# Cross-attention and a dequantised feed-forward on one core: the first block's steps in a new order, and three of down's integer steps in earlier rounds

## The chip, the core and the metric

The kernel runs on one core of a Trainium2 chip. The metric is the device time of one execution in microseconds; it is given as the median of several runs. The engines are PE (matrix products, with PEld for its weight loads), DVE (vector work), ACT (activation functions, scaled copies), POOL (general elementwise work, and one queue of transfers) and SP (a second queue of transfers).

## What is computed

`x` has 32 batches of 64 rows and 512 columns, and so has the context. First comes cross-attention. Its "channels" are the 64 rows of a batch; the 512 columns are cut into 8 heads of 64. Then comes a gated feed-forward over the 512 columns, whose three weights are stored as integers 0 to 15 with a zero point and a scale for each group of 128 input rows. Both parts add to `x`.

```python
h = layernorm(x)                                   # over 512 columns
q, k, v = Wq@h + bq, Wk@ctx + bk, Wv@ctx + bv      # 64x64 weights, per batch
p = softmax(q_head @ k_head.T / 8)                 # 64x64 per batch and head
x = x + Wo @ concat(p @ v_head) + bo
W = (integers - zeros) * scales                    # gate, up: 512x1792; down: 1792x512
h = layernorm(x)
x = x + (silu(h @ W_gate) * (h @ W_up)) @ W_down
```

## The kernel before

**Tiling.** Two batches make a pair: 128 partitions of 512 columns. Two pairs make a set, four pairs a block, and there are four blocks. The feed-forward of a block works on 512 columns (its 4 x 128 rows, transposed). The normalised input is held transposed in a high half `hTh` and a low half `hTl`, and each product is taken with both halves. The 1792 inner columns are 14 chunks of 128. Gate and up of a chunk take four groups `g` of 128 input rows. Between the groups ACT multiplies the running sum in PSUM by a quotient of two scales (`s_q`, line 670), so the weights stay integers less their zero points. Down adds each chunk's product to `y` on DVE, times a scale (line 718); it has four column tiles `l` per chunk, and only two PSUM banks (`ps_d`) for these products.

**Getting the weights.** Integers come by POOL's queue (`load_wide`, line 271, `load_down`, line 275), in four column ranges `wide`: 0 to 256, then three of 512. Zero points come as broadcasts by SP's queue (`load_zeros`, `load_down_zeros`). POOL subtracts zeros from gate and up (`weight_steps`, line 309), DVE from down (`down_steps`, line 322).

**The first block.** Its attention and second normalisation run pair by pair before any feed-forward product, in the order of the string `START` (line 796): each word is a step of a pair ("2.scores") or a shared step. `tc.manual_schedule()` keeps each engine's instructions in that order. The steps of a pair are: `stats`, `scale`, `apply` (mean and variance on DVE, inverse root on POOL, normalise on DVE at line 112); `q`, `k`, `v` products and `q_out`, `k_out` (add the bias from PSUM on DVE, line 450), `v_out` (ACT); `scores`, `highest`, `less`, `exp`, `sums`, `divide` (the softmax: PE, DVE, DVE, ACT, DVE, POOL); `turn`, `turn_out`, `weigh` (products with Wo and v); `residual` (line 568: two DVE operations of 128x256, product + bias + x, then a store to `x1_dram`); `stats2`, `scale2`, `apply2`, `flip` (transpose), `high` (ACT), `low` (DVE). `warm` is a pair of products with no use but to keep PE running. Shared steps: `gate`, `up`, `more_gate`, `more_up` issue weight loads, `integers` does one subtraction of 256 columns on POOL, `zeros`, `broadcast`, `more` bring the zero points, `scales` and `quotients` build `s_q`. "behind products" ties a transfer to the last product traced before it.

**The rounds.** After that come 28 rounds per block (line 938 on). A round advances two chains of gate and up, one step of the next block's attention (`ROUND_STEPS`; for the next two blocks' sets the names end in `_4to`, `_6to`, and so on), and down, which lags by 6 rounds and does two of its four column tiles twice per round. `LOADS_AT` names the rounds that load weights, `WEIGHTS_AT` those in which POOL subtracts, `DOWN_AT` those in which DVE subtracts the zeros of one more chunk of down. A planner then sets each engine's order from its own estimates; `tc.issue_after` holds some instructions behind the newest one traced on their engine.

Of the kernel before, what the change touches and what calls it, by code (L numbers as in the profile page):

```python
# [9 lines left out]
F32 = mybir.dt.float32  # L10
# [16 lines left out]
def kernel(  # L27
# [88 lines left out]
    with ExitStack() as fast:  # L116
# [118 lines left out]
            yield  # L235
            nc.scalar.copy(s_all, pS)

        def quotients():

            s_inv = early.tile([P, 2, NS - FC], F32, tag="s_inv", name="s_inv")  # L240
            later = s_all[:, 0:2, FC:]
            nc.vector.scalar_tensor_tensor(s_inv, later, 0.0, later, ALU.is_equal, ALU.add)
            nc.vector.reciprocal(s_inv, s_inv)
            nc.vector.tensor_tensor(s_q, s_all[:, 0:2, : NS - FC], s_inv, ALU.mult)

        def last_quotients():

# [102 lines left out]
        class Attention:  # L350
# [61 lines left out]

            stats2, scale2 = stats, scale

            def apply2(self):

                if not PB <= self.p < 2 * PB:
                    return self.apply()
                less = small.tile([P, self.n], F32, tag="less", name=f"less_{self.name}")
                nc.vector.scalar_tensor_tensor(  # L420
                    less, self.mv[:, :, 0], -1.0, self.rs, ALU.mult, ALU.mult
                )
                for i in range(self.n):
                    nc.scalar.activation(
                        self.at["xn"][:, i, :],
                        self.x[:, i, :],
                        AF.Identity,
                        bias=less[:, i : i + 1],
                        scale=self.rs[:, i : i + 1],
                    )  # L430

# [22 lines left out]

            def k_out(self):
                self.with_bias("k_eT", self.pk, 1)

            def q(self):
                self.pq = self.heads("xn", WQ, "pq")
# [103 lines left out]

            def residual(self):
                x_heads = self.by_head(self.x)
                for h in range(2):
                    x_h = x_heads[:, :, h, :]
                    nc.vector.scalar_tensor_tensor(
                        x_h, self.po[:, h, :, :], bvo[:, 1:2], x_h, ALU.add, ALU.add
                    )  # L570
                nc.sync.dma_start(x1_dram[:, self.p : self.p + self.n, :], self.x)


            def flip(self):
                two = self.tile("ph")[:, : self.n, :]
                self.ph = two.rearrange("p i (c d) -> p c i d", d=P)
                for i in range(self.n):
                    for c in range(KT):
                        nc.tensor.transpose(
                            self.ph[:, c, i, :], self.at["xn"][:, i, ts(c, P)], ident  # L580
                        )

# [206 lines left out]
        def chain(*gens):  # L789
# [4 lines left out]


        START = """
            0.stats 0.scale 0.apply 1.stats projections 1.scale biases
            projections_out 1.apply 2.stats 0.k biases_out 2.scale 3.stats 0.q 1.q
            0.k_out 3.scale 0.q_out 1.k zeros 1.q_out 0.scores 1.k_out 2.k 3.apply
            1.scores broadcast 0.highest 2.apply 2.k_out 0.less 0.v 1.highest 0.exp  # L800
            2.q 1.less 0.v_out 3.q 0.sums 1.exp 2.v 2.q_out 0.divide 3.k gate
            2.v_out 1.sums 2.scores 3.q_out 1.divide 3.k_out 1.v 2.highest 3.scores
            1.v_out 2.less 1.turn 3.highest 2.exp 0.turn up rows 3.less 1.turn_out
            2.sums 3.exp 1.weigh 0.turn_out 3.sums 2.divide 3.v 1.residual 1.stats2
            3.divide integers integers integers integers 0.weigh 3.v_out 2.turn
            0.residual 0.stats2 1.scale2 more_gate integers 3.turn more 2.turn_out
            2.weigh 3.turn_out 1.apply2 0.scale2 integers integers scales 2.residual
            2.stats2 3.weigh scales_out 1.flip 2.warm 3.residual 3.stats2 3.warm
            3.warm 2.scale2 integers 1.high 0.apply2 3.scale2 more_up 2.apply2
            0.flip 1.low 2.flip 3.apply2 0.high quotients 3.flip 3.warm 2.high 0.low  # L810
            3.high 2.low 3.low
        """
        place = places(att)
        with (
# [44 lines left out]
            for step in START.split():  # L859
                if step[0].isdigit():  # L860
                    getattr(pairs[int(step[0])], step[2:])()
                elif step == "zeros":
                    zeros_to_dram()
                elif step == "broadcast":
                    with behind_products():
                        early_zeros.append(load_zeros(*wide[0], early))
                elif step == "gate":
                    with behind_products():
                        load_wide(ng, gate_rows, *wide[0])
                elif step == "up":  # L870
                    with behind_products():
                        load_wide(nu, up_rows, *wide[0])
                elif step == "rows":
                    with behind_products():
                        load_rows(PB // SET)
                elif step == "more":
                    with behind_products():
                        early_zeros.append(load_zeros(*wide[1]))
                elif step == "more_gate":
                    load_wide(ng, gate_rows, *wide[1])  # L880
                elif step == "more_up":
                    load_wide(nu, up_rows, *wide[1])
                    load_down(0, wide[1][0] + wide[1][1])
                elif step == "integers":
                    next(weights)
                elif step == "quotients":
                    quotients()
# [47 lines left out]
        with ExitStack():  # L935
            for r in range(NBLK * ROUNDS + LAG):
# [163 lines left out]
```

## Time and profile before

| what | value |
|---|---|
| three runs | 437.92 us median (437.63 to 438.35) |
| the profiled execution | 437.77 us, its span 436.0 us |
| PE busy in the span | 406.6 us (93%) |
| DVE, ACT, POOL busy | 327.9, 307.7, 281.1 us |
| first product of the feed-forward | starts at 39.54 us |
| mean granted PE clock | 0.992 |

All times of the profile count from the start of the span; about 1.8 us of the execution lie outside it. In a table by stage the columns are: the stage, its length, each engine's busy time with its number of instructions, the granted PE clock as a share of full speed, the share of time that the transfer engines were busy, and GB/s. A line of a timeline is: start, duration, engine, source line, operation, output and inputs with their shapes, the count, and in brackets the idle time before it and what ended that. Consecutive instructions of an engine overlap, so the next one starts some 0.1 us before the last one's end.

### The profile page before, as it was taken

To read this page: it belongs to the slowest core of one execution; us is meant where nothing else is said; L and a number is where in the kernel's file an instruction comes from. 1 tells how busy PE (TensorE), PEld (TensorE's weight loads), DVE (VectorE), ACT (ScalarE), POOL (GpSimd) and SP (SyncE) were. 2 spreads that over 40 slices of the span, in tenths; PEclk is the share of its full clock that TensorE was granted. 3 is DMA by queue.
4 is the path that set the end of the run, shared out by engine and by line. 5 is a ranking of instruction groups with operands and counts; after the bars stand their busy time and mean duration, and the time that the engine had idled before them with its cause. 6 is when DMAs were issued, how large, how long until landed. Compare 5 with 4: busy or idle time off the path is not lost. (4 is left out here: it accounts for less than half of the span.)

```text
span 436.0 us, 10361 instructions
## 1 busy us (share of the span) xinstructions
PE 406.6 (93%) x4191; PEld 312.6 (72%) x4191; DVE 327.9 (75%) x513; ACT 307.7 (71%) x472; POOL 281.1 (64%) x291
## 2 busy tenths in 40 slices
PE   4767989899999999999999999989999999999993
PEld 3555657567777776877778787767778888887772
DVE  4988766997788874895779785896869656768675
ACT  2243888476978589766988579666788778777771
POOL 4384948867645446675778668775787887774330
PEclk9999989999999999999999999999999999999998
DMA  7299648951021200411010102300000013110002
GB/s 214 63 301 370 209 126 284 322 187 50 2 74 50 98 2 0 146 51 51 0 50 1 51 2 98 112 34 2 2 37 15 1 49 98 59 39 0 2 4 100
DMA packets 20911, 36.54 MB, mean 84 GB/s; under 512 B 1832, under 2 KB 7416, under 8 KB 20856
## 3 DMA queue, kind: packets, MB, share of 16 engines
q1 hardware_dynamic: 14056, 24.20, 16.6%
q0 software_dynamic: 6192, 11.01, 8.4%
q8 instruction: 35, 0.57, 0.5%
q10 hardware_dynamic: 608, 0.59, 0.4%
q14 instruction: 20, 0.16, 0.1%
HBM read 27.37 MB, written 8.42 MB: 82 GB/s over the span
## 5 line engine op out<-in xcount | busy, mean ns | idle before, releaser
L718 DVE SCALAR_TENSOR_TENSOR y<-pd,s_all,y 128x512 f32<-128x512 f32 x204 | 150.0, 743 | 43.2 <-PE pd L708 39.8
L670 ACT ACTIVATE pg<-pg,s_q 128x512 f32<-128x512 f32 x168 | 111.7, 666 | 67.0 <-PE pg L660 65.9
L670 ACT ACTIVATE pu<-pu,s_q 128x512 f32<-128x512 f32 x168 | 111.2, 663 | 8.0 <-PE pu L660 6.9
L686 POOL CAST hh<-h 128x512 fp32r<-128x512 f32 x55 | 37.0, 673 | 100.4 <-DVE h L676 89.1
L705 PE MATMUL pd<-hh,nd 128*128 128x512 f32 x224 | 93.2, 416 | 2.3 <-DVE y L718 1.6
L660 PE MATMUL pg<-hTh,ng 128*128 128x512 f32 x224 | 90.3, 403 | 3.2 <-DVE hTl L602 1.6
L660 PE MATMUL pu<-hTh,nu 128*128 128x512 f32 x224 | 90.7, 405 | 1.4 <-POOL nu L309 1.1
L660 PE MATMUL pg<-hTl,ng 128*128 128x512 f32 x224 | 89.3, 399 | 0.0
L660 PE MATMUL pu<-hTl,nu 128*128 128x512 f32 x224 | 89.1, 398 | 0.0
L708 PE MATMUL pd<-hl,nd 128*128 128x512 f32 x224 | 88.8, 396 | 0.0
L687 POOL TENSOR_TENSOR hl<-h,hh 128x512 fp32r<-128x512 f32 x55 | 72.7, 1321 | 4.2
L676 DVE SCALAR_TENSOR_TENSOR h<-pu,s_all,g 128x512 f32<-128x512 f32 x56 | 41.8, 747 | 29.7 <-ACT g L673 19.6
L339 POOL TENSOR_TENSOR squares<-squares 128x512 f32<-128x512 f32 (+1 forms) x46 | 55.1, 1198 | 1.7
L705 PEld LDWEIGHTS pd<-hh,nd 128*128 128x128 f32 x224 | 42.0, 188 | 18.0 <-DVE y L718 5.2
L660 PEld LDWEIGHTS pg<-hTh,ng 128*128 128x128 f32 x224 | 42.3, 189 | 16.9 <-ACT pg L670 2.6
L660 PEld LDWEIGHTS pu<-hTh,nu 128*128 128x128 f32 x224 | 42.3, 189 | 16.6 <-ACT pu L670 2.0
L660 PEld LDWEIGHTS pg<-hTl,ng 128*128 128x128 f32 x224 | 42.4, 189 | 9.5
L660 PEld LDWEIGHTS pu<-hTl,nu 128*128 128x128 f32 x224 | 42.4, 189 | 9.4
L673 ACT ACTIVATE g<-pg,s_all 128x512 f32<-128x512 f32 x56 | 39.0, 697 | 13.6 <-PE pg L660 12.1
L708 PEld LDWEIGHTS pd<-hl,nd 128*128 128x128 f32 x224 | 42.1, 188 | 8.3 <-issue 0.4
L309 POOL TENSOR_TENSOR nu<-nu,z 128x512 fp32r<-128x512 f32 (+1 forms) x16 | 17.5, 1095 | 3.0 <-DMA nu<-in_L_ffn_up_w_dram 2.9
L309 POOL TENSOR_TENSOR ng<-ng,z 128x512 fp32r<-128x512 f32 (+1 forms) x16 | 16.7, 1050 | 2.4 <-DMA ng<-in_L_ffn_gate_w_dram 2.4
(295 smaller groups left out, 464.9 us busy)
## 6 DMA issues: line engine op xcount, KB each, us to landing
c_set<-in_ctx_dram SPq DMA_DIRECT2D x6, 512.0 KB
x<-in_x_dram SPq DMA_DIRECT2D x6, 512.0 KB
z<-z_dram SPq DMA_DIRECT2D x6, 512.0 KB
ng<-in_L_ffn_gate_w_dram POOLq DMA_DIRECT2D x3, 1024.0 KB, 7.1
nu<-in_L_ffn_up_w_dram POOLq DMA_DIRECT2D x3, 1024.0 KB, 8.0
x_dram<-x SPq DMA_DIRECT2D x6, 512.0 KB
r<-x_dram SPq DMA_DIRECT2D x6, 512.0 KB
out_dram<-r SPq DMA_DIRECT2D x6, 512.0 KB
```

Source lines behind the costliest of these rows:

```text
L309: nc.gpsimd.tensor_tensor(piece, piece.bitcast(F32), z16[:, m, g, :], ALU.subtract)
L339: nc.gpsimd.tensor_tensor(total[:, :n], total[:, :n], square[:, :n], ALU.add)
L660: nc.tensor.matmul(acc, w[:, g, ts(f, P)], half[:, g, :], start=(g == 0 and half is hi), stop=(g == KT - 1 and half is lo), skip_group_che ...
L670: nc.scalar.activation(acc, acc, AF.Copy, scale=by)
L673: nc.scalar.activation(g_sb, acc, AF.Silu, scale=by)
L676: ins = nc.vector.scalar_tensor_tensor(h_sb, acc, by, g_sb, ALU.mult, ALU.mult)
L686: nc.gpsimd.tensor_copy(hh, h_sb)
L687: ins = nc.gpsimd.tensor_tensor(hl, h_sb, hh.bitcast(F32), ALU.subtract)
L705: nc.tensor.matmul(pd, w, h_hi[t, f], start=(t, f) != LAST, stop=False, skip_group_check=True)
L708: nc.tensor.matmul(pd, w, h_lo[t, f], start=False, stop=True, skip_group_check=True)
L718: ins = nc.vector.scalar_tensor_tensor(y, pd, by, y, ALU.mult, ALU.add)
```

## The change

Two changes are made at once.

*The first block.* `START` is a new order: pairs go 0, 2, 1, 3 for much of it, and the queries are computed before the keys for pair 0. The work of some steps goes to other engines. Pairs 2 and 3 are normalised by POOL (`apply_pool`). Their keys are copied from PSUM by ACT (`k_copy`), and POOL adds the bias (`k_bias`). The output bias is added to `x` early, by ACT (`shift`), so that the residual is one DVE operation of 128x512. The second normalisation is done by ACT in the first block too (`apply2`, line 424 before), after a small DVE operation (`less2`). The quotients' guards against zero are two POOL operations, and the quotients of the first two chunks are made in the first block, those of the other twelve after round 1. The transposes of `flip` are kept together. The eight `integers` are spread differently, and all four subtractions of up's first columns stand directly before `more_up`.

*Down's integers.* The steps of chunks 3, 4 and 5 are taken in rounds 8, 8 and 9; before they were in rounds 9, 11 and 13. The order listing of the two programs shows on DVE: chunks 3 and 4 now stand before the second y of chunk 1, chunk 5 behind h of chunk 3. On SP the zero broadcast for chunks 6 to 9 now stands before a store of `x`. On PE the order of the rounds is the same up to the fourth down product of chunk 3, which now comes earlier; a few products behind it change places.

```diff
-        def quotients():
-            s_inv = early.tile([P, 2, NS - FC], F32, tag="s_inv", name="s_inv")
+        s_inv = const.tile([P, 2, NS - FC], F32, tag="s_inv", name="s_inv")
+        def guards():
             later = s_all[:, 0:2, FC:]
-            nc.vector.scalar_tensor_tensor(s_inv, later, 0.0, later, ALU.is_equal, ALU.add)
-            nc.vector.reciprocal(s_inv, s_inv)
-            nc.vector.tensor_tensor(s_q, s_all[:, 0:2, : NS - FC], s_inv, ALU.mult)
+            nc.gpsimd.tensor_scalar(s_inv, later, 0.0, None, ALU.is_equal)
+            nc.gpsimd.tensor_tensor(s_inv, s_inv, later, ALU.add)
+        def quotients(fs: slice):
+            for m in range(2):
...
+                nc.vector.reciprocal(inv, inv)
+                newest["DVE"] = nc.vector.tensor_tensor(quot, num, inv, ALU.mult).ins
...
+            def apply_pool(self):
+                nc.gpsimd.tensor_scalar(
+                    self.at["xn"][:, 0, :], self.x[:, 0, :], self.mv[:, 0, 0:1], self.rs,
+                    ALU.subtract, ALU.mult)
+            def less2(self):
+                self.less = small.tile([P, self.n], F32, tag="less", name=f"less_{self.name}")
+                nc.vector.scalar_tensor_tensor(
+                    self.less, self.mv[:, :, 0], -1.0, self.rs, ALU.mult, ALU.mult)
             def apply2(self):
-                if not PB <= self.p < 2 * PB:
+                if self.p >= 2 * PB:
                     return self.apply()
...
+            def k_copy(self):
+                nc.scalar.copy(self.by_bank("k_eT"), self.pk)
+            def k_bias(self):
+                k = self.by_bank("k_eT")
+                b = bqk[:, 1, :].unsqueeze(1).unsqueeze(1).to_broadcast([P, 2, self.n * KT, D])
+                nc.gpsimd.tensor_tensor(k, k, b, ALU.add)
...
             def residual(self):
                 x_heads = self.by_head(self.x)
+                if self.n == 1:
+                    x_h = x_heads.rearrange("p n h d -> p h n d")
+                    nc.vector.tensor_tensor(x_h, self.po, x_h, ALU.add)
+                    return self.keep_rows()
...
+            def shift(self):
+                nc.scalar.activation(self.x, self.x, AF.Identity, bias=bvo[:, 1:2])
...
         START = """
...
+            0.stats 0.scale 0.apply projections 1.stats biases projections_out
+            1.scale 2.stats 0.q biases_out 0.shift 3.stats 2.scale 0.k 2.apply_pool
+            0.q_out 2.k 0.k_out 3.scale 2.shift 2.q 1.apply 3.apply_pool 2.k_copy
+            0.scores 2.q_out 1.shift 1.k 0.highest zeros 3.shift 0.less 1.q 2.k_bias
+            broadcast 1.k_out 0.exp 3.k 1.q_out 2.scores 3.k_copy 0.sums 1.v 3.k_bias
+            2.highest 3.q 1.v_out 1.scores 2.less 0.divide gate 3.q_out 2.exp 0.v
+            1.highest 0.turn 0.v_out 3.scores 0.turn_out 1.less 2.sums 1.exp 2.v 3.v
+            2.v_out 3.highest 2.divide up rows 0.weigh 3.v_out 3.less 1.sums 3.exp
+            2.turn 2.turn_out 3.sums 1.divide 2.weigh 0.residual 3.divide 1.turn
+            2.residual scales 1.turn_out 2.stats2 integers 3.turn more scales_out
+            integers 1.weigh 3.turn_out 0.stats2 2.scale2 3.weigh 0.warm integers
+            2.less2 3.residual 2.apply2 0.scale2 3.stats2 2.flip integers 2.high
+            more_gate 0.less2 1.residual 0.apply2 guards 1.stats2 0.flip 1.warm
+            3.scale2 0.high 2.low 1.scale2 3.less2 integers 1.less2 3.apply2 0.low
+            integers 1.apply2 quotients 3.flip integers 3.high 1.flip integers 3.low
+            1.high more_up 1.low 1.warm
...
-        DOWN_AT = [4, 5, 6, 14, 22] + [2 * f + 3 for f in range(2, FC)]
+        DOWN_AT = {4: 1, 5: 1, 6: 1, 7: 1, 8: 2, 9: 1, 14: 1, 22: 1}
+        DOWN_AT |= {2 * f + 3: 1 for f in range(6, FC)}
...
-                    if r in DOWN_AT:
-                        advance(down_weights)
+                    advance(down_weights, DOWN_AT.get(r, 0))
...
+                if r == 1:
+                    with tc.issue_after(newest["DVE"]):
+                        quotients(slice(FIRST // P, FC))
```

More of the change, by code (lines that the diff above doesn't have):

```diff
@@ L236, in scales @@
             nc.scalar.copy(s_all, pS)
-        def quotients():
-            s_inv = early.tile([P, 2, NS - FC], F32, tag="s_inv", name="s_inv")
+        s_inv = const.tile([P, 2, NS - FC], F32, tag="s_inv", name="s_inv")
+        def guards():
             later = s_all[:, 0:2, FC:]
-            nc.vector.scalar_tensor_tensor(s_inv, later, 0.0, later, ALU.is_equal, ALU.add)
-            nc.vector.reciprocal(s_inv, s_inv)
-            nc.vector.tensor_tensor(s_q, s_all[:, 0:2, : NS - FC], s_inv, ALU.mult)
+            nc.gpsimd.tensor_scalar(s_inv, later, 0.0, None, ALU.is_equal)
+            nc.gpsimd.tensor_tensor(s_inv, s_inv, later, ALU.add)
+        def quotients(fs: slice):
+            for m in range(2):
+                inv, num, quot = (
+                    a.rearrange("p (g f) -> p g f", f=FC)[:, :, fs]
+                    for a in (s_inv[:, m, :], s_all[:, m, : NS - FC], s_q[:, m, :])
+                )
+                nc.vector.reciprocal(inv, inv)
+                newest["DVE"] = nc.vector.tensor_tensor(quot, num, inv, ALU.mult).ins
         def last_quotients():
@@ L413 @@
             stats2, scale2 = stats, scale
+            def apply_pool(self):
+                nc.gpsimd.tensor_scalar(
+                    self.at["xn"][:, 0, :],
+                    self.x[:, 0, :],
+                    self.mv[:, 0, 0:1],
+                    self.rs,
+                    ALU.subtract,
+                    ALU.mult,
+                )
+            def less2(self):
+                self.less = small.tile([P, self.n], F32, tag="less", name=f"less_{self.name}")
+                nc.vector.scalar_tensor_tensor(
+                    self.less, self.mv[:, :, 0], -1.0, self.rs, ALU.mult, ALU.mult
+                )
             def apply2(self):
-                if not PB <= self.p < 2 * PB:
+                if self.p >= 2 * PB:
                     return self.apply()
[L419 to L422, printed above, removed]
+                if self.n > 1:
+                    self.less2()
                 for i in range(self.n):
@@ L427, in apply2 @@
                         AF.Identity,
-                        bias=less[:, i : i + 1],
+                        bias=self.less[:, i : i + 1],
                         scale=self.rs[:, i : i + 1],
@@ L570, in residual, with keep_rows @@
                     )
+                self.keep_rows()
+            def keep_rows(self):
                 nc.sync.dma_start(x1_dram[:, self.p : self.p + self.n, :], self.x)
+            def shift(self):
+                nc.scalar.activation(self.x, self.x, AF.Identity, bias=bvo[:, 1:2])
             def flip(self):
@@ L576, in flip @@
                 self.ph = two.rearrange("p i (c d) -> p c i d", d=P)
[L577 to L581, printed above, removed]
+                with self.in_order() as first_taken:
+                    for i in range(self.n):
+                        for c in range(KT):
+                            nc.tensor.transpose(
+                                self.ph[:, c, i, :], self.at["xn"][:, i, ts(c, P)], ident
+                            )
+                            first_taken()
             def warm(self):
@@ L796 @@
         START = """
[L797 to L808, printed above, removed]
@@ L809 @@
-            3.warm 2.scale2 integers 1.high 0.apply2 3.scale2 more_up 2.apply2
-            0.flip 1.low 2.flip 3.apply2 0.high quotients 3.flip 3.warm 2.high 0.low
-            3.high 2.low 3.low
+            0.stats 0.scale 0.apply projections 1.stats biases projections_out
+            1.scale 2.stats 0.q biases_out 0.shift 3.stats 2.scale 0.k 2.apply_pool
+            0.q_out 2.k 0.k_out 3.scale 2.shift 2.q 1.apply 3.apply_pool 2.k_copy
+            0.scores 2.q_out 1.shift 1.k 0.highest zeros 3.shift 0.less 1.q 2.k_bias
@@ L886 @@
                 elif step == "quotients":
-                    quotients()
+                    quotients(slice(0, FIRST // P))
+                elif step == "guards":
+                    guards()
                 elif step.endswith("_out"):
```

## The prediction

> **What bounds the kernel now.** I read the page's slices first, then busy time by stage, then the timelines of PE, VectorE (DVE) and GpSimd (POOL) from 0 to 112 us. The chain of work that ended last says nothing here: it holds only the last 0.4%.
>
> ```profile
> core 0: us, PE busy (x) PEld busy (x) DVE busy (x) ACT busy (x) POOL busy (x), PEclk, DMA share, GB/s
> 0.00:39.50 39.50, 24.84 (x717) 19.75 (x717) 32.21 (x72) 12.10 (x22) 22.03 (x41) 1.00 0.71 219
> 39.50:110.00 70.50, 66.08 (x754) 47.01 (x755) 53.17 (x75) 50.28 (x75) 51.27 (x49) 0.98 0.65 206
> 110.00:400.00 290.00, 286.70 (x2592) 223.55 (x2591) 218.74 (x334) 226.22 (x345) 200.19 (x196) 1.00 0.13 42
> ...
> 60.00:63.40 3.40, 3.40 (x9) 2.49 (x9) 2.76 (x6) 2.20 (x5) 2.12 (x2) 0.51 0.18 44
> ```
>
> From 110 us on PE is 99% busy, so a shift of PE's position at 110 us moves the end by as much. Up to 39.5 us DVE is the full engine (32.2 us, with 1.9 us of gaps from 8.5 us on) and ACT the empty one (12.1). Between them lie about 4.4 us of PE gaps, and one stretch at half clock (last row).
>
> ```profile
> 39.54 0.47 PE L660 MATMUL pg<-hTh,ng 128*128 128x512 f32 x1 [1.56 <-DVE hTl L602]
> ...
> 47.14 1.48 PE L438 MATMUL pq_4to<-w_T,xn_set 64*64 64x64 f32 x64
> ...
> 69.51 0.50 PE L705 MATMUL pd<-hh,nd 128*128 128x512 f32 x1
> ...
> 83.41 0.50 PE L705 MATMUL pd<-hh,nd 128*128 128x512 f32 x1 [1.28 <-DVE y L718]
> ...
> 89.36 0.49 PE L660 MATMUL pu<-hTh,nu 128*128 128x512 f32 x1 [0.84 <-POOL nu L309]
> ```
> ```profile
> 37.41 1.88 DVE L602 TENSOR_TENSOR hTl<-ph,hTh 128x512 fp32r<-128x512 f32 x3
> ...
> 45.19 2.68 DVE L112 TENSOR_SCALAR xn_set<-x,mv_4to,rs_4to 128x512 f32<-128x512 f32 x2 [2.09 <-POOL rs_4to L402]
> ...
> 66.46 1.85 DVE L322 TENSOR_TENSOR nd<-nd,z 128x512 fp32r<-128x512 f32 x1
> 68.23 0.57 DVE L398 TENSOR_SCALAR rs_6to<-mv_6to 128x2 f32<-128x2 f32 x1
> 68.72 1.40 DVE L718 SCALAR_TENSOR_TENSOR y<-pd,s_all,y 128x512 f32<-128x512 f32 x2
> ```
> ```profile
> 35.19 0.81 POOL L273 DMA_DIRECT2D nu<-in_L_ffn_up_w_dram  x1
> ...
> 43.31 1.17 POOL L309 TENSOR_TENSOR nu<-nu,z 128x512 fp32r<-128x512 f32 x1 [2.94 <-DMA nu<-in_L_ffn_up_w_dram]
> 44.43 0.72 POOL L402 TENSOR_TENSOR rs_4to<-rs_4to,nhalf 128x2 f32<-128x2 f32 x1
> ...
> 65.83 1.93 POOL L529 TENSOR_TENSOR q_e_set<-q_e_set,sm_4to 128x1024 f32<-128x1024 f32 x1
> ```
>
> What to see: the first gate product (39.54) follows DVE's last low half (37.41 + 1.88 = 39.29) by 0.25. The second set's queries (47.14) hang on a DMA: nu's second columns land at 43.3, POOL subtracts, POOL takes the root (44.43), DVE normalises (45.19), and PE, free at 47.05, starts at 47.14. So this chain is already just in time. And the fourth down product of chunk 1 (69.51) starts as DVE's y (68.72 + 0.74 = 69.46) ends: also just in time.
>
> **The first block, step by step.** Durations are start to start in a full queue. DVE gives up: two normalisations (pairs 2, 3; 0.46 each, 0.9), two key biases (0.60 each, 1.2), four second normalisations (0.46 each, 1.8), half of each residual (0.82 for two 128x256 becomes one 128x512 from PSUM like L450's 0.60: 0.9), and 0.65 of the quotients (1.15 becomes four tiny operations, 0.5). It gains four "less" of 128x1; the near row is L420 (128x2): 0.15 alone, 0.40 beside POOL; I take 0.25, 1.0 in all. Net 4.5 us off DVE.
>
> The work goes to ACT and POOL. ACT: four bias shifts (near row: exp 128x512, 0.63), two key copies (0.57), four normalisations (L424: 0.82), 7 us into an engine 27 us idle. POOL: two normalisations, two key biases (near row L529: 1.05 each) and two guard operations of 84 columns (0.3 each from L309's 0.66 for 256 columns), 4.8 us into an engine 17 us idle. Bounds for the unshown POOL normalisation: 0.61 (cast row) to 2.0. A rule speaks against this move: the Trainium skill's "GPSIMD Engine Reference", section 4, wants elementwise work on VectorE, because GpSimd takes about twice as long for two inputs. The rows agree on the price (1.05 against 0.60). By the rule alone the two biases and two normalisations would cost 2 us more than they save; by the rows of the queues they replace time of the full engine by time of one that waits 6.2 us before its first division (18.40). With 2.0 us each the walk below ends 0.6 later, no more.
>
> I then walk the new order forward, each engine in its own order, each step at the latest of its inputs and its engine. The same walk over the old order gives 39.13 for the last low half (trace 39.29), so I add 0.16. New stations: first scores at 12.3 as before; last softmax sums at 23.7 (before 25.1); residuals of pairs 0 and 2 at 24.9; pair 3's at 28.1, pair 1's at 30.3; pair 1's statistics at 31.4 (+1.10), root 32.05 (+0.56), less 32.9, ACT's two normalisations 33.4 and 34.1 (0.82, 0.72 apart), transpose 34.75, high half 35.4, low half 36.1. Plus 0.16 and 0.25: first gate product at 36.5, **3.0 us earlier** (2.2 if every less waits 0.65 for POOL, 3.8 if none waits). 1.5 of the 4.5 stay as new DVE waits: the end is now a chain through ACT. The transfers that these steps issue move with them: first gate columns 19.4 to 17.8, first up columns 23.3 to 21.8, ng's second columns 29.5 to 28.6, all on POOL's queue behind products that end earlier; the stores of the residuals on SP's. The remaining quotients (0.9 in round 1) lie in DVE's idle 2.09 before 45.19.
>
> **Does the start survive the second set?** With 3.0 off, PE wants the queries at 44.1. The chain from nu's landing to PE was 47.14 - 43.31 = 3.8, so nu must land by 40.3. Its issue hardly moves (35.19 to 34.6: four subtractions at 0.64 now stand right before it). What changes is the traffic before it. In the old trace the zero broadcast (1 MB, issued at 28.15) ran until 34 at 0.2 MB/us, POOL's queue moved nothing from 29 to 33, ng landed at 39.1, nu took 4.1 more. In the new order the broadcast stands behind pair 3's turn (25.7 instead of 27.2) and earlier stores: issued at 25.8, done near 32; ng then needs 1 MB at 0.4 MB/us plus 0.5 MB of stores and rows: near 36; nu (and half of a row load) 1.3 to 1.5 MB more: 39.5 to 41. I take 40.3: the 3.0 just survives. Bounds: 39.5 (no wait) to 43.3 (all is given back).
>
> **Down's integers.** Chunks 3 to 5 leave rounds 9, 11, 13 for 8, 8, 9. In DVE's order two now stand before the y at 68.72, one behind h_3. Each costs 0.60 free, but chunk 2 beside POOL's division cost 1.85; I take 1.2 to 1.9 for both. Queued behind them: y of chunk 1, whose bank PE's product at 69.51 awaits. There is no cover (0.05 us), ACT is not behind there either (idle 1.00 before 70.75), so PE stands **1.55 us**. SP's order: the broadcast for the next down zeros moves ahead of a store, but its data dependence (chunk 5, round 9) is over before; no cost. Given back: chunk 4 (0.66 at 81.97) no longer precedes the y that PE awaits at 83.41, worth 0.45 after PE's new order there (a down product comes earlier), and chunk 5 (1.73 at 86.55, beside POOL) no longer stretches nu's subtraction from 1.17 to 1.60, so the two waits on nu (0.84, 0.22) shrink; the second ends about 0.65 earlier than before, the 0.45 included. Net **0.9 lost** (0 to 1.6).
>
> **The half-clock stretch.** From 60.0 to 63.4 eight products start 0.43 apart instead of 0.23: 1.6 us, after 56.6 to 60.0 with PE busy 1.87 of 3.40. "TensorE: Matmul & The Clock Gate", Part 1, says the clock is judged in free-running windows of 3.4 us, so a shift of 3 us makes this stretch a matter of luck: by the rule alone I would credit about 0.8. By the trace the stretch is there, and three times within 0.72 us say that it is there in every run, which a random phase would not give. I keep it, as a case of its own.
>
> **The sum.** 437.77 (span 436.0 plus 1.8 around it) - 3.0 + 0.9 = 435.7; the median of the runs is 0.15 higher: **435.8**.
>
> **Rivals.** (a) As forecast, 434.8 to 437.0 with its own bounds, 0.42. (b) The half-clock window no longer covers PE's gaps at 57 to 60: another 1.6 off, 434.2; 0.25. For it: the gap (2.9 us) nearly fills one window; against: the equal runs. (c) nu lands near 42, because row loads of the third and fourth set share the transfers: 1.3 remains of the start, minus 0.9: 437.5; within 0.2%; 0.15. (d) Slower, one mechanism: nu lands as late as before. It decides from 42.4 on, where what is left of the start equals the 0.9 of the down integers. PE then waits over 2 us at the queries, and such a gap in 3.4 us is what preceded the half clock, so 1.6 is added: at 42.8, 437.9 - 0.5 + 0.9 + 1.6 = 439.9; 0.18. For it: the issue time does not move. Against: the broadcast does.
>
> **Chances.** Faster: (a), (b) and a little of (c), 0.70; within 0.2% (0.9 us, about what a measurement here can tell from no change) 0.13; slower 0.17. The range 433.8 to 438.7 takes in (a) to (c) with their bounds (3.8 at the start; 1.6 at the integers) and leaves out most of (d).
>
> **What would show it.** First gate product near 36.5; nu's first subtraction of 512 columns near 40.3 and the queries near 44; the product at 69.51, shifted by 3, with a wait for y of 1.2 to 1.9; waits at 83.41 and 89.36 shorter; granted clock 0.5 once between 56 and 61. I am wrong if the first product comes after 37.3, if nu lands after 42, or if chunks 3 and 4 find a hole that I do not see.

## The result, and the profile after

The changed kernel takes 441.35 us in the median of 20 runs (438.41 to 442.73), the kernel before 438.26 in 20 runs beside it: ratio 1.0049 (95% interval 1.0031 to 1.0067), so **slower by 0.5%**. The forecast was 435.8 us, range 433.8 to 438.7. The profiled execution took 441.92 us (before 437.77), its span 440.1. Ratios, here and below, leave out runs more than 1.5% above the fastest of their kernel, which concerns four runs of one kernel (`loads_early`), its profiled one among them. They are measured against runs of the kernel before on the same chip, and are not the quotients of two medians.

The same table by stage as before, then the stretches that turned out to matter:

```profile
core 0: us, PE busy (x) PEld busy (x) DVE busy (x) ACT busy (x) POOL busy (x), PEclk, DMA share, GB/s
0.00:39.50 39.50, 24.73 (x705) 21.13 (x705) 26.72 (x60) 17.27 (x30) 27.39 (x44) 0.87 0.70 202
39.50:110.00 70.50, 64.03 (x710) 44.38 (x712) 51.12 (x80) 49.28 (x75) 49.77 (x48) 0.98 0.72 216
110.00:400.00 290.00, 286.69 (x2645) 224.27 (x2635) 219.13 (x330) 225.00 (x343) 202.27 (x197) 1.00 0.12 42
25.00:36.00 11.00, 8.46 (x171) 7.09 (x171) 6.25 (x16) 3.07 (x6) 6.19 (x11) 0.54 0.85 241
60.00:63.40 3.40, 2.36 (x9) 0.99 (x7) 3.23 (x5) 3.37 (x6) 0.00 (x0) 1.00 0.67 210
73.60:77.30 3.70, 3.70 (x11) 2.88 (x10) 1.79 (x3) 2.42 (x4) 3.10 (x3) 0.54 1.30 348
```

VectorE did lose work: 32.2 us up to the first gate product became 28.6 (26.7 of them by 39.5 us, the table's first row). That is 3.6 less, where the forecast took 4.5. But PE's clock is at half for most of 25 to 36 us, where it was full before; the stretch from 60.0 to 63.4 is at full clock now, and another, from 73.6, is at half. PE's timeline shows where the start went (the number in brackets is the idle time before the line):

```profile
21.25 0.43 PE L588 MATMUL po<-v_set,k_eT_set 64*64 64x64 f32 x14
23.98 0.50 PE L588 MATMUL po<-v_set,k_eT_set 64*64 64x64 f32 x18 [2.29 <-issue]
...
27.91 0.58 PE L571 MATMUL pe<-w_T,q_e_set 64*64 64x64 f32 x9
29.91 0.81 PE L571 MATMUL pe<-w_T,q_e_set 64*64 64x64 f32 x20 [1.42 <-issue]
...
41.97 0.47 PE L706 MATMUL pg<-hTh,ng 128*128 128x512 f32 x1 [0.74 <-DVE hTl L648]
...
49.58 1.16 PE L462 MATMUL pq_4to<-w_T,xn_set 64*64 64x64 f32 x64
...
72.87 0.50 PE L751 MATMUL pd<-hh,nd 128*128 128x512 f32 x1 [2.23 <-DVE y L764]
...
87.55 0.50 PE L751 MATMUL pd<-hh,nd 128*128 128x512 f32 x1 [0.62 <-DVE y L764]
...
93.77 0.49 PE L706 MATMUL pu<-hTh,nu 128*128 128x512 f32 x1 [0.39 <-POOL nu L319]
```

PE stops twice in the middle of a row of like products whose inputs are all there ("issue": it waited for nothing that the profile shows). The first gate product comes at 41.97 instead of 39.54 (forecast 36.5), the queries at 49.58 instead of 47.14, and the wait for y is 2.23 us. On POOL (one line) and DVE:

```profile
9.42 2.08 POOL L426 TENSOR_SCALAR xn_set<-x,mv,rs 128x512 f32<-128x512 f32 x1
...
14.20 0.39 POOL L153 CAST z<-z_nat 56x256 bf16<-56x256 int32 x1
...
45.32 1.16 POOL L319 TENSOR_TENSOR nu<-nu,z 128x512 fp32r<-128x512 f32 x1 [2.94 <-DMA nu<-in_L_ffn_up_w_dram]
```
```profile
23.75 0.20 DVE L557 RECIPROCAL sm<-sm 128x8 f32<-128x8 f32 x1
...
67.62 1.15 DVE L332 TENSOR_TENSOR nd<-nd,z 128x512 fp32r<-128x512 f32 x1
68.69 1.86 DVE L408 TENSOR_SCALAR rs_6to<-mv_6to 128x2 f32<-128x2 f32 x1
70.47 1.69 DVE L332 TENSOR_TENSOR nd<-nd,z 128x512 fp32r<-128x512 f32 x2
72.08 1.40 DVE L764 SCALAR_TENSOR_TENSOR y<-pd,s_all,y 128x512 f32<-128x512 f32 x2
```

A normalisation on POOL takes 2.08 us, at the upper bound of the forecast (2.0); the zero casts come at 14.20 instead of 11.56. Yet the last softmax sums are there at 23.75, where the forecast had them (23.7). What fails is on PE.

### The profile page after: what moved, and what is told of

It is laid out like the page before. It is cut to its first block, busy times and chain, and to the rows that moved or that the text cites. A ratio compares the mean times of both kernels' runs of the same rounds, so it can differ in the third digit from the quotient of the medians.

```text
span 440.1 us, 10375 instructions
## 1 busy us (share of the span) xinstructions
PE 408.3 (93%) x4187; PEld 314.9 (72%) x4187; DVE 324.2 (74%) x510; ACT 314.2 (71%) x482; POOL 289.0 (66%) x297
## 4 chain that ended last, share of the span: by engine, by line
PE 69%; DVE 9%; POOL 8%; ACT 6%; issue 4%; DMA 3%; SPq 0%; POOLq 0%; DVEq 0%; ACTq 0%
PE pg L706 19%; PE pu L706 19%; PE pd L751 10%; PE pd L754 9%; DVE y L764 3%; DMA z<-z_dram 2%; POOL hl L733 1%; POOL squares L349 1%; PE py L779 1%; DMA x<-in_x_dram 1%; ACT q_e_set L552 1%; DVE q_e_set L539 1%; DVE nd L332 1%; POOL squares L347 1%; POOL q_e_set L562 1%
```

## The experiments

Theory 1: both parts lose. In the first block PE stands for its own instructions, because their fetch is held up by transfers; in the rounds, the two subtractions before y cost more than the forecast's 1.55. Rivals: only one part loses; POOL's 2.08 us do it; the half clock alone does it. The tables give each kernel's median, its ratio to the kernel before, and what its profile shows. "nu lands" is the start of POOL's first subtraction of 512 columns of nu, "queries" the first product of the second set's queries. A profile is one execution only, and need not be like the median run.

### One part at a time

`start_only` is the changed kernel with

```diff
-        DOWN_AT = {4: 1, 5: 1, 6: 1, 7: 1, 8: 2, 9: 1, 14: 1, 22: 1}
-        DOWN_AT |= {2 * f + 3: 1 for f in range(6, FC)}
+        DOWN_AT = {r: 1 for r in [4, 5, 6, 14, 22] + [2 * f + 3 for f in range(2, FC)]}
```

> The new first block with down's integer steps in their old rounds. Theory 1 (both parts lose): the start is as in the changed kernel, first gate product at 41 to 42.5 us with two stalls of PE in the middle of products (about 2.3 and 1.4 us), 69.5's down product 1.2 late, end 1 later than before: 439.3, and the stall of 2.2 us before the down product of chunk 1 is gone. Rival (only down's integers lose): 437 or less, first product near 37 to 39. Rival (half clock alone is to blame): first product late in this run only if the granted clock falls to 0.5 between 26 and 36 us.

`down_only` is the kernel before with the new `DOWN_AT`.

> The old first block with down's integer steps in the new rounds. Theory 1: PE stands 1.5 to 2.2 us before the fourth down product of chunk 1 at about 69.5, and a stretch at half clock of 3.4 us follows it (1.6 more); 0.9 is given back at 83 and 89: 440.5 to 441.5. Rival (the forecast's sizes): stall 1.55, no new half clock, 0.65 given back: 439.2. Rival (it costs nothing, all of the loss is the start's): 438.3.

| kernel | median us | ratio (95%) |
|---|---|---|
| start_only | 439.35 | 1.0019 (1.0003 to 1.0035) |
| down_only | 439.79 | 1.0024 (1.0007 to 1.0041) |

Each part loses 0.2%, and the two add up to the 0.5%. start_only's profile has its first product at 42.32 and one stop of 2.95 us, after nine products of pair 1's turn, the place of the 1.42 above; the other stop is absent. down_only waits 2.08 us for y, and its clock is at half from 73.2 to 76.6.

### Is it POOL's lateness?

`norm_dve`: start_only with `2.apply_pool` and `3.apply_pool` replaced by `2.apply` and `3.apply`. `zeros_early`: start_only with `zeros` moved in front of `3.apply_pool`.

> start_only with pairs 2 and 3 normalised by VectorE again (0.46 us each, at the same places of the order), so GpSimd has no step of 2.08 us. Theory 1 (GpSimd's lateness puts the zero broadcast into the row and weight loads, and PE's instruction fetches stand behind them): zero casts near 11.9, broadcast issued near 14.5 instead of 17.8, no stall of PE over 0.5 us in the middle of products between 20 and 31 us, first product at 36.9 to 38: 435.5 to 437. Rival (PE reaches its fetches sooner in the new order whatever the transfers do): a stall of about 2 us stays near 21 to 24, first product 41, 439. Rival (half clock alone): depends on the clock of that run only.

> start_only with GpSimd's two zero casts moved ahead of its second normalisation (that of pair 3), nothing else. Theory 1: the casts run at 11.5 to 12.8 and the broadcast is issued near 14.5 to 15.5, GpSimd still has its two steps of 2.08 us; the stalls in the middle of products go or fall under 0.7 us in sum, first product 37 to 38.5: 435.5 to 437.5. Rival (GpSimd's 2.08 us steps themselves delay PE by the key biases): pair 3 is 0.7 later still, first product 41 to 42.5, 439 to 440. Rival (fetches fall in the dense stretch anyway): stalls stay, 439.

| kernel | median us | ratio (95%) | zero casts | stops over 0.4 us from 17 us on | first product |
|---|---|---|---|---|---|
| norm_dve | 438.63 | 1.0019 (0.9994 to 1.0045) | 11.02 | 1.16, 0.63, 1.26 | 38.88 |
| zeros_early | 437.46 | 0.9980 (0.9955 to 1.0004) | 12.56 | 1.83 | 41.07 |

The stops stay though the broadcast goes out 2 to 3 us earlier than in the changed kernel (17.78), at 14.42 and 15.71. So this half of the theory falls: PE stops without POOL's long steps and without the late broadcast. norm_dve, which has neither, has the same ratio as start_only, so the price of these steps alone isn't it either. But the order of POOL's work is not free: zeros_early lies 0.39% below start_only by the ratios, some 1.7 us (the two intervals barely touch). Which way that gain comes about is not shown.

The half clock alone falls too: in the changed kernel the stop that ends at 23.98 is over before the half clock begins at 25.9, and loads_early2 below has a stop of 1.55 us at full clock.

### Are the stops instruction fetches?

In the first block of all traces of the new order (without added products), stops come only after PE products number 219, 346, 472 and 598, that is, 126 or 127 apart, whatever the products are. With its weight load each product is two instructions, so 126 of them are some 250 instructions; and the queue that the profile calls "instruction" moves one 16 KB packet per such block. Shifting the stream must shift the stops. `pad64` and `pad32` put small products with unused results into PE's first idle time:

```diff
+            for i in range(32):                      # 64 in pad64
+                b, h = i // 2 % 2, i % 2
+                nc.tensor.matmul(spare[ts(h, D), b, 5 * D : 6 * D],
+                                 ident[ts(b, D), :D], ident[ts(b, D), :D], start=True, stop=True)
```

> start_only with 64 small products more on PE in its first idle time (before the projections' transposes, which wait for a load until 5 us or later), results unused. They cost no time there but shift every later instruction by 64 products. Theory (the stops in the middle of products are instruction fetches, one per 126 products): the stop after nine products of pair 1's turn is gone, and a stop appears 64 products earlier in the stream, inside the products that were numbers 534 (a weigh) and perhaps 408 and 660. Rival (the stop belongs to those products, a wait that the trace does not show): it stays after nine products of pair 1's turn, 1.3 to 3 us long. Time 437.5 to 440 in both.

> As pad64, with half as many: 32 small products, each of which counts as two in the trace, so PE's stream is shifted by 64. (The 64 of pad64 were 128 in the trace, that is one whole block, so that run could not tell the two apart.) Theory (instruction fetches, one per 126 products): no stop after nine of pair 1's turn (number 598 of start_only, here 662); stops over 0.25 us in the middle of products only at numbers near 534 and 660 less 64 of shift counted from start_only's 472 and 598, that is inside a weigh (start_only's 534, here 598), and perhaps where start_only has 408 or 660. Rival (it belongs to those products): a stop of 1 to 3 us stays after nine of pair 1's turn.

pad64 (439.49 us, ratio 1.0032, 1.0015 to 1.0049) was a miss: a product counts twice in the trace, so the shift was 128, just one block, and the stop stayed in place (1.57 us). 36 packets were moved instead of 34 or 35. pad32 (444.0 in its one run) tells the two apart; its PE timeline:

```profile
24.25 0.46 PE L598 MATMUL po<-v_set,k_eT_set 64*64 64x64 f32 x14 [0.75 <-ACT k_eT_set L591]
26.32 0.50 PE L598 MATMUL po<-v_set,k_eT_set 64*64 64x64 f32 x17 [1.61 <-issue]
...
27.59 0.81 PE L581 MATMUL pe<-w_T,q_e_set 64*64 64x64 f32 x32
```

The stop is now inside a weigh, at product 600, and pair 1's turn (27.59) runs through. Its smaller stops, 0.51 and 0.56 us, are at 473 and 726, again 126 or 127 away. So the stops belong to the instruction stream, not to those products. The fetch itself, in the changed kernel's transfers for the two stretches 24.0 to 27.4 us and 27.4 to 28.6 (queue, its packets, MB, share of the engines; the shares add up to more than 100% because the recorded times of packets overlap):

```profile
q0 software_dynamic: 725, 0.72, 91.0%
q1 hardware_dynamic: 287, 0.56, 47.1%
```
```profile
q1 hardware_dynamic: 147, 0.27, 62.2%
q0 software_dynamic: 93, 0.08, 35.3%
q8 instruction: 1, 0.02, 6.0%
```

PE enters the block from product 472 at 23.98. The packet for the block behind it runs only at 27.43 to 28.58, while the other queues fill the engines, and PE resumes 1.33 us after that, at 29.91.

### Do transfers hold the fetch?

`loads_late` is zeros_early with the next set's rows and context behind the products near 27 us; `loads_early` is norm_dve with those rows issued at 11 us and the first columns of gate and up at 15 us, before the busy time; `loads_early2` also moves the second zero broadcast forward (it goes out at 21.05); `before_early` makes the moves of loads_early in the kernel before. In words of `START`:

```diff
-   ... up rows 0.weigh ...  integers 3.turn more ...
+   ... up 0.weigh ...  integers 3.turn more rows context ...   (loads_late)
-   ... 0.k 2.apply ...  zeros 3.shift ...  0.divide gate ...  up rows 0.weigh
+   ... 0.k rows 2.apply ...  zeros gate up 3.shift ...  0.divide ...  0.weigh   (loads_early)
+   ... 0.divide more 3.q_out ...                                (loads_early2, besides)
```

> zeros_early with two loads of the next set (its rows, 0.5 MB, and its context, 0.5 MB) tied behind the weigh and turn products near 27 us instead of going out at 20 and 22 us. In zeros_early PE crosses into the instruction block that begins at product 472 near 22 us, the fetch of the next block runs only at 26.1 to 27.1, and PE stops at product 598 for 1.83 us. Theory (the transfers in the queues hold the fetch back): the fetch runs within 2 us of the crossing, by 24.5, the stop at product 598 falls under 0.6 us, first gate product 1 to 1.5 earlier than in zeros_early, 436 to 437 us in the median if the late loads are not missed by the second set. Rival (a block of 126 products can't be had faster than every 4.5 us, whatever else is in the queues): stop of 1.3 us or more stays, time as zeros_early, 437.5.

> norm_dve with three loads moved from 19 to 22 us into the quiet time of the transfers from 9 to 15 us: the next set's rows (behind pair 0's keys), the first columns of gate and of up (right behind the zero casts). Theory (transfers hold PE's fetches, and the forecast's walk of the order was right but for them): no stop in the middle of products over 0.6 us from 20 us on, first gate product 36 to 37.5, and ng's and nu's second columns land no later than before (nu by 42), so that the queries start by 46 and a gain of 1 to 2.5 stays: 435.5 to 437. Rival (fetch speed is set by the block, not by traffic): stops of 0.6 and 1.3 as in norm_dve, first product 38.9, 438.6. Rival (start gained but the second set gives it back): first product near 36.5, queries after 47.5, 438.3.

> loads_early, and the second zero broadcast (1 MB, needed only by the second columns) goes out behind pair 1's scores near 18 us instead of near 28. Theory (nu's landing, the chain into the second set's queries, is limited by what lies before it in the transfers): nu lands 1 to 2 us earlier than in loads_early, by 41, queries by 45: 434.5 to 436. Rival (the broadcast now lies across the fetches at 19 to 24 us): a stop of 1 us or more is back, first product 38 or later, 438 or more.

> The kernel before, in its old order, with the same three loads moved to the quiet time as in loads_early. Theory (the old order leaves its fetches enough time and waits on VectorE, so earlier transfers gain nothing at the start; PE is free for the queries only at 47): first product 39.2 to 39.8, 437.5 to 438.3, no change. Rival (early loads help by themselves, whatever the order): 436.5 or less.

| kernel | median us | ratio (95%) | stops | first product | nu lands | queries |
|---|---|---|---|---|---|---|
| loads_late | 438.85 | 1.0007 (0.9989 to 1.0026) | none | 36.50 | 45.19 | 48.60 |
| loads_early | 441.57 | 1.0038 (1.0013 to 1.0063) | none | 38.65 | 47.93 | 51.31 |
| loads_early2 | 440.99 | 1.0044 (1.0022 to 1.0067) | 1.55 | 39.96 | 47.57 | 50.96 |
| before_early | 438.12 | 0.9985 (0.9962 to 1.0008) | 1.07, 1.08, 0.64 | 40.13 | 43.42 | 47.73 |

Without the two loads the stops are gone, and the first product comes at 36.50, where the forecast put it. But the second set gives it back: nu lands at 45 to 48, and in loads_late PE waits 1.78 us for the context:

```profile
36.50 0.47 PE L706 MATMUL pg<-hTh,ng 128*128 128x512 f32 x1 [0.77 <-DVE hTl L648]
...
39.45 1.98 PE L462 MATMUL pk_4to<-w_T,c_set 64*64 64x64 f32 x64 [1.78 <-DMA c_set<-in_ctx_dram]
```

In loads_early the rows of the *third and fourth* set now go out at 35.91, in front of nu (issued at 37.12). before_early shows fetch stops in the old order too (at products 347, 473 and 600), but under waits for VectorE, and the time is the same. One comes there even with the loads in their old places: down_9_10 below, whose first block is the old one, stops for 0.94 us at product 600, and its first product is at 39.07 nevertheless.

### Is the gain always given back?

Here those later rows are held behind the products of rounds 2 and 3. `norm_held`, `zeros_held`, `before_held` and `after_held` are norm_dve, zeros_early, the kernel before and zeros_early with the new `DOWN_AT`, all with

```diff
-        for j in range(PB // SET + 1, 2 * PB // SET + 1):
-            load_rows(j)
+                if r in ROWS_AT:                      # {2: PB // SET + 1, 3: PB // SET + 2}
+                    with behind_products():
+                        load_rows(ROWS_AT[r])
```

`plan` adds to norm_held the early rows, and `gate up` directly behind `3.scale`; `rows_early_held` adds to zeros_held only the early rows.

> norm_dve with the row loads of the third and fourth set (two of 0.5 MB, at 38 to 39 us there) tied behind the products of rounds 2 and 3, past 43 us. Theory (these rows delay nu's landing, which sets the second set's queries): nu lands by 41.5 instead of 42.8 and, in runs where it was later, not after 43; queries by 46.5, the slow half of norm_dve's runs (441.7 to 442.4) is gone: median 436.5 to 437.3. Rival (nu is limited by its own queue, whatever SP's queue moves): nu at 42.8 or later, 438.6.

> zeros_early with the same two row loads held back. Theory: the fetch stop near 28 us stays (1.8 us, first product 39.5 to 41), the second set is not limiting then, so little changes: 437 to 437.5. Rival (rows delay the second set there too): 436.3 or less.

> norm_dve with the next set's rows, the first gate and up columns in the quiet time from 10 to 15 us (the two weight loads now ahead of GpSimd's zero casts, so that its key bias is not behind a wait for PE), and the rows of the third and fourth set held back. Theory (both limits of the early start are transfers: fetches at 20 to 30 us, nu at 36 to 45): no stop in the middle of products over 0.6 us from 20 us on, first product 36.5 to 37.5, nu by 41, queries by 45: 435 to 436.5, faster than both kernels. Rival (the early start is always given back): queries at 47 or later, 438.3 or more.

> The kernel before with the same two row loads held back. Theory (the old order's queries start as PE comes free, 47.05, so nu's earlier landing gains nothing): 437.8 to 438.3, and none of the runs above 440 in which nu is late. Rival (the rows delay its second set as well): 437 or less.

> zeros_held with the next set's rows (0.5 MB) loaded behind pair 0's keys, at about 11 us, instead of at 22 us. Theory (less traffic while the block from product 472 is fetched): that fetch runs within 2 us of the crossing, no stop over 0.6 us at product 598 in the profile, median 435.7 to 436.4. Rival (the traffic that is moved delays the fetches at 14 to 18 us instead, as in plan): a stop of 1 us or more at product 346, 436.7 or more.

| kernel | median us | ratio (95%) | stops | first product | nu lands | queries |
|---|---|---|---|---|---|---|
| norm_held | 437.08 | 0.9971 (0.9953 to 0.9988) | 0.73, 2.35 | 41.68 | 44.40 | 49.29 |
| zeros_held | 436.67 | 0.9955 (0.9939 to 0.9971) | none | 36.56 | 41.41 | 44.81 |
| plan | 438.51 | 0.9993 (0.9972 to 1.0013) | 2.61 | 38.73 | 44.73 | 48.13 |
| before_held | 437.70 | 0.9979 (0.9964 to 0.9993) | none | 39.03 | 42.66 | 46.63 |
| rows_early_held | 436.07 | 0.9949 (0.9917 to 0.9980) | none | 36.23 | 42.66 | 46.05 |

zeros_held and rows_early_held beat the kernel before by 0.5%, and the changed kernel by about 1%. Holding the rows back is worth 0.48% from norm_dve to norm_held (7 of norm_dve's 22 runs took 441.65 us or more, the slowest of norm_held 441.14). From zeros_early to zeros_held it is 0.25%, where the intervals overlap.

zeros_held was expected to change little, since I took the stop of zeros_early's one profile for granted. Its own profile has no stop over 0.4 us, though its program is the same up to there: the stops come in some executions and not in others. Its PE timeline is the forecast of the first block come true, with 0.17 us left of the stop:

```profile
26.22 0.52 PE L571 MATMUL pe<-w_T,q_e_set 64*64 64x64 f32 x20 [0.17 <-issue]
...
36.56 0.47 PE L706 MATMUL pg<-hTh,ng 128*128 128x512 f32 x1 [0.78 <-DVE hTl L648]
...
44.81 0.69 PE L462 MATMUL pq_4to<-w_T,xn_set 64*64 64x64 f32 x32 [0.57 <-DVE xn_set L112]
```

This profile (434.7 us) is the fastest of 18 runs, that of norm_held (441.14) the slowest of 22, and that of norm_dve, with its three stops, the fastest of 22 (435.96). So how often the median run stops, and what the stops cost in it, is not shown. rows_early_held, which was to spare the fetch, differs from zeros_held by less than the intervals.

plan missed: its early loads lie across the fetch at 14 to 18 us, and the stop moved there (2.61 us at product 346). before_held was expected to change nothing and gained a little; one profile doesn't say where.

The times of all these fetches, worked out from the packets' records in the traces (from PE's entry into the block at 472 to the packet that fetches the block from 598, and the stop at 598):

| the loads of rows and context | fetch begins after, us | stop, us |
|---|---|---|
| both at 19 to 23 us: start_only, zeros_early, after, norm_held, after_held, norm_dve, zeros_held | 4.47, 3.74, 3.46, 3.34, 2.67, 2.38, 2.17 | 2.95, 1.83, 1.42, 2.35, 1.58, 1.26, none |
| the broadcast in their place: loads_early2 | 3.24 | 1.55 |
| one or none: loads_early, rows_early_held, plan, loads_late | 1.99, 1.97, 1.44, 1.16 | none |

With the same arithmetic the fetch behind product 219 begins 3.46 us late in plan and 3.11 in before_early (the loads moved there), and 0.24 to 1.63 in the others. Within one program the lag varies as well (3.74 in zeros_early, 2.17 in zeros_held), and the two groups of loads lie close (2.17 and 1.99), so the rows say that heavy transfers go with late fetches, with one profile for each kernel; they give no threshold. In the kernel before the block from 473 on takes PE 4.1 us, and its fetch begins after 1.62, lasts 0.96 and is of use some 1.4 later: 4.0, just in time. PE runs there through product 600:

```profile
26.52 0.69 PE L538 MATMUL pe<-w_T,q_e_set 64*64 64x64 f32 x32 [0.31 <-POOL q_e_set L529]
27.04 0.65 PE L555 MATMUL po<-v_set,k_eT_set 64*64 64x64 f32 x32
```

### Down's integers

`down_9_10` and `down_8_11` are the kernel before with

```diff
+        DOWN_AT = {4: 1, 5: 1, 6: 1, 7: 1, 9: 2, 10: 1, 14: 1, 22: 1}            # down_9_10
+        DOWN_AT = {4: 1, 5: 1, 6: 1, 7: 1, 8: 1, 11: 1, 13: 1, 14: 1, 22: 1}     # down_8_11
```

> The old first block; down's integers of chunks 3, 4, 5 in rounds 9, 9, 10, so that on VectorE two stand behind h of chunk 3, none before the second y of chunk 1. Theory (the loss of down_only is the two steps before that y): no wait of PE near 69.5 us, no half-clock stretch after it, waits at 83.41 and 89.36 shorter by 0.6 and 0.4: 437.3 to 437.8. Rival (what is given back is not real, or two behind h_3 delay y just as well): 438.3 or more, with a wait of 0.6 us or more for a y near 71 to 73.

> The old first block; only chunk 3 earlier, in round 8 (one step before the second y of chunk 1), chunks 4 and 5 in their old rounds 11 and 13. Theory (a step before that y costs PE its whole length, with no cover): PE waits 0.5 to 1.2 us at about 69.5, too short to bring a half-clock stretch, nothing is given back: 438.8 to 439.5. Rival (it is the pair of steps, or GpSimd's division beside them, and not the place): under 0.3 us of wait, 438.3.

> The changed kernel with the zero casts ahead of pair 3's normalisation on GpSimd and the rows of the third and fourth set held back to rounds 2 and 3; it is zeros_held with down's integers in rounds 8, 8, 9. Theory (the parts add; two subtractions before the second y of chunk 1 cost 1.6 us and now and then a stretch at half clock, 0.9 comes back later): a wait of 2.0 to 2.3 us for y at about 67 to 69, 1.2 to 2 us over zeros_held: 437.9 to 438.7. Rival (with an earlier start PE has room there): within 0.5 of zeros_held, 437.

| subtractions before the second y | kernels | wait of PE for y, us |
|---|---|---|
| none | before, then down_9_10, zeros_held, start_only | 0.05, then 0.46, 0.49, 0.60 |
| one | down_8_11 | 1.05 |
| two | down_only, after_held, after | 2.08, 2.11, 2.23 |

Each subtraction costs its 0.6 to 0.8 (two from 70.47 to 72.08 in the changed kernel), without cover. A further 0.4 to 0.6 is not theirs: in 16 of the 20 profiles, start_only's among them, the small `rs_6to` operation takes 1.86 us beside POOL's division, and in that of before only 0.57. down_8_11 takes 438.80 (1.0018, 1.0000 to 1.0035), as expected; down_9_10 takes 440.0 (1.0045, 1.0017 to 1.0073), a miss. There the wait only moved, as its DVE timeline shows:

```profile
79.08 3.48 DVE L322 TENSOR_TENSOR nd<-nd,z 128x512 fp32r<-128x512 f32 x1
82.49 0.74 DVE L718 SCALAR_TENSOR_TENSOR y<-pd,s_all,y 128x512 f32<-128x512 f32 x1
```

Chunk 5's subtraction, 0.67 us when alone, takes 3.48 beside POOL's subtractions for gate and up, and PE waits 2.46 us for the y behind it. after_held (439.86; 1.0019, 0.9996 to 1.0043) lies 0.64% above zeros_held by the ratios, 2.8 us, more than expected; its profile has a stop of 1.58 us in the first block, so a part of that may be the start's chance. The rival, that the second part costs little where the start is early, falls: the difference is above its 0.5.

## Why the prediction was wrong

**POOL's normalisation**: taken at 1.05, is 2.08; the rule that the forecast set against it speaks of two inputs, and this operation has one. The step "with 2.0 us each the walk ends 0.6 later, no more" is not contradicted: the softmax sums were on time, and norm_dve, which takes these operations away, has no better ratio.

**First gate product at 36.5: failed by 5.5 us**, and this is the main error. The walk moved each step to "the latest of its inputs and its engine" and took PE as ready to issue whenever inputs are. It put the supply of PE's instructions at nothing. They arrive in blocks of 126 products, each of use 4.5 to 7.0 us after PE entered the last one where transfers were dense (begin of the fetch, its 1.0, and some 1.4), while PE in the new order needs 3.9 to 4.3 for it (zeros_held). The two stops are 3.7 us. The rest, an estimate: products at half clock from 25.9 to 36.2 (63 of a weigh 2.19 us, against 0.65 for 32 before: 0.9; a transpose 1.06 against 0.63; 20 of a turn 0.81 against 0.52 in loads_early2), together 1.6. In loads_late, zeros_held and rows_early_held, without stops, it came at 36.50, 36.56 and 36.23 (in loads_early, also without stops, at 38.65, after PE had waited 2.29 us up to 17.68 for a key bias by POOL): the walk's end was right to 0.3, though VectorE's busy time before it fell by 3.5 us and not by 4.5 (32.2 to 28.7 in zeros_held). That transfers hold the fetch is supported by moving them, in one profile each: the stops went with the loads to another block (plan) or away (loads_late). Which part of the queues does it is open.

**nu by 40.3, queries at 44.1**: 45.32 and 49.58, so by the point named ahead ("after 42") wrong. The chain nu, root, normalise, queries is as told; it was not the limit in the changed kernel's profile, whose start was already late (the first product and the queries by 2.4, nu by 2.0). Where the start was early it did limit: 41.41 and 44.81 in zeros_held, with a wait of 0.57 before the queries. So rival (d) has a real mechanism, and it costs time in the median too, as the rows held back show (0.48% in norm_held). It isn't what the changed kernel's profile shows.

**The half clock**: kept at 60.0 to 63.4 for all runs, because "three times within 0.72 us say that it is there in every run". Wrong: down_only has it at 32.2 to 35.6 and 73.2 to 76.6, before_held at 31.0 to 34.4, before_early and zeros_held nowhere before the end. The stretches last 3.4, 6.8 or 10.2 us and often come after PE stood; PE's standing does not bring one each time (after_held waits 2.11 us without one). The three near-equal times were luck: 20 runs of the same kernel go from 436.63 to 441.63. The rule of the Trainium skill's "TensorE: Matmul & The Clock Gate", Part 1, that the windows run free, was the better guide. In the changed kernel it went from 60 (1.6 us won) and came at 73.6 (1.6 lost) and at 25.9.

**Down's integers**: right in mechanism (y stands behind two subtractions, no cover, PE waits) and near in size: the two take 1.61 (70.47 to 72.08), forecast 1.55. The other 0.6 of the wait of 2.23 is `rs_6to` beside the division, which most kernels have without the change, so part of it lies in the profile before, where it happened to be short. Given back was 0.9, not 0.65: the waits of 1.28 and 0.84 are 0.62 and 0.39, and one of 0.22 is 0.45. From profile to profile the forecast's net 0.9 became 1.3, without the half clock; the medians say 1.1 (0.3 to 1.8) for down_only.

**The sum**: +2.1 us by the ratio instead of -2.1. The start missed by 3.8 (start_only: +0.8 against -3.0), the integers by about 0.2, which is within their interval. Of the 3.8, moving the zero casts ahead won back 1.7 and holding the rows back another 1.1 (start_only to zeros_early to zeros_held, by ratios that are each known to 0.7 to 1.1 us). How much of the 3.8 the stops make in the median run is open; in the profile they are 3.7 of the 5.5 us at the first product. The forecast's range did not take in rival (b) with all of its bounds (434.2 - 0.8 - 0.9 = 432.5), though it said so; nothing turned on that.

## What to carry to other kernels

A walk of dependences through a dense row of small products needs one more resource: the instruction stream. Count PE's instructions per microsecond, find the "instruction" packets among the transfers, and look for "issue" gaps in the middle of like products; a new order that makes PE denser at a moment of heavy loads can get stuck there, in some executions and not in others. Rows that nobody needs yet should be held back: that won 0.48% in norm_held. And a stretch at half clock in one profile is not a property of the kernel, even if the runs beside it agree.

## What was not expected of the hardware

- PE fetches 16 KB of instructions per 126 products of its 64x64 kind. The packet takes 0.9 to 2.0 us, begins, in the first block, up to 4.5 us after PE enters its block, and after a stop PE resumes 1.3 to 1.6 us after its end.
- The same program has the stop in one execution and not in another (zeros_early 1.83 us, zeros_held 0.17, with equal instructions up to there).
- POOL's subtract-and-multiply of 128x512 by two values per partition takes 2.08 us; operations there with two inputs of that size take 1.03 to 1.74 over all profiles, the same normalisation on DVE 0.54.
- VectorE's operations stretch beside POOL's: a subtraction of 0.67 us took 3.48 (down_9_10), and one of 128x2 elements 1.86 instead of 0.57.
